# An AdaLN block with Mamba-2 layers and a mixture of experts: all input loads moved to the first slots of the DMA queue, the blank rows of the expert lists to later ones

## The chip, the core and the metric

The kernel runs on one core of a Trainium2 chip. A core has five engines with an instruction stream of their own each: PE (TensorE, matrix products), DVE (VectorE), ACT (ScalarE), POOL (GpSimd) and SP (SyncE), which here does nothing but issue transfers (DMAs). Transfers from SP, ACT and POOL stand in queues of their own and are carried out by 16 DMA engines that all queues share. Each engine takes its instructions in the order of the program; engines wait for one another, and for transfers, by semaphores. The metric is the time of one execution on the device, in microseconds (us); below are medians of several runs.

## The reference

Eight sequences (B=8) of 512 tokens (L) with 128 features (DM). Each goes through a modulated layer norm, four Mamba-2 layers with residuals, and a second modulated norm with a mixture of experts (8 experts, the best 2 for each token, and a shared one):

```python
mod = (silu(c) @ wmod).reshape(8, 6, 1, -1)       # sa, ca, ga, sb, cb, gb
h = layernorm(x) * (1 + ca) + sa
for l in range(4):                                # Mamba-2 layer
    z, xBC, dt = split(rmsnorm(h, w[l]) @ W_in[l])
    xBC = silu(causal_conv4(xBC, conv_w[l]) + conv_b[l])
    xs, Bm, Cm = split(xBC)
    dt = softplus(dt + dt_bias[l]); A = -exp(A_log[l])
    state = state * exp(dt * A) + (dt * xs) x Bm  # scan over 512 steps
    y = state . Cm + D[l] * xs
    h = h + rmsnorm(y * silu(z), gate_w[l]) @ W_out[l]
x = x + ga * rmsnorm(h, final_w)
h = layernorm(x) * (1 + cb) + sb
x = x + gb * (shared_expert(h) + top2_of_8_experts(h))
```

## The kernel before

**Tiles and units.** A sequence's input is one tile of 128 partitions by 4 chunks by 128 features (256 KB). One layer of one sequence is a unit, 32 in all (layer by layer, all eight sequences in each), and a unit has four chunks of 128 tokens (NC=4). The scan is done in chunks: 128 *items*, each one chunk of one unit, with a 128x128 decay matrix per head (the tile `dV`, 512 KB). Decay rows are computed for two units at a time (a group, eight items), stored to DRAM (`crow`), and loaded back broadcast over the partitions (`dV` and `ecum`).

**One hand-written order.** The whole scan part is one loop over *slots*, `for t in range(-NC * LEAD - EARLY, NI + 4)`, with `p = t + 16`. It runs from p=-9 (t=-25) to t=131. What a slot emits is each engine's order, and nothing is rearranged. In slot t are, among others: item t's products and state, the elementwise work of item t+1 to t+3, the loads of item t+4 (`decay_rows`, the `dV` load on SP), the projection and convolution of tile p, and one step of each generator in `gens`, in the order in which they were put there. A generator is a piece of work cut by `yield` into steps of one slot.

**Names in the prediction.**
- `enter(b)` (line 608) is the generator that takes sequence b in. It starts at p = 4b-9: x load on SP (line 613); a slot later the product `pmA` of `scb` and the modulation weights `wm` on PE (616), which ACT copies to `md` (618, 619), then layer norm: statistics on DVE (164, 166), the inverse root on POOL (149, 150), scaling (ACT line 181, or POOL 172), times scale and plus shift (185, 186), sums of squares on ACT (155), inverse root on POOL, normalizing (203 on ACT, or 201 on POOL: `hnA`), transposing on PE (208), and ACT's copy to `hT` (210). Sequences 1 to 4 use POOL for most of it (`idle`), the others ACT and DVE.
- `project_x` (PE, 638) writes tile `px` into one of three PSUM banks; `conv_first` (ACT, 650) and, a slot later, three taps `conv_tap` (DVE, 660) make `xbc` of it. `silu` (ACT, 672, 673) finishes a unit.
- `softplus_a` to `sums_b` (lines 693 to 767) make the decay of a group; line 765 stores `crow`. `decay_rows` (779 and 786) loads it, `decay_diff` on POOL (793) is the first to use a `dV` tile. There are six `dV` buffers, so that SP's load of item t+4 waits until PE has used the tile of item t-2 (line 920).
- `load_small()` (117) is a generator of three steps: `dtb`, `negA`; then four loads of `Dch` and `gw`; then `fw` and the FFN's norm weight. It starts at p=-4.
- `load_weights(l)` (595) loads `Wi` and `Wo` of a layer on SP, the first at p=-8. ACT's queue has the loads of `cT` and `wm` (92, 93), POOL's those of `bw`, `cw` and `cbias` (94 to 96).
- `clear_lists()` (243) writes blank rows into the lists `xg` of the experts in DRAM, from a tile `blank`: 64 transfers of 260 KB and one of 130 KB on SP. It starts at p=-2 (t=-18). The first 36 go out three a slot, to p=9; the other 29 one a slot, from p=10 to p=38 (t=22).
- `prepare_experts` (255), from p=0, computes modulations for the second half and loads its small parameters. `scale_weights(l)` (601, POOL) scales `Wo` in every 32nd slot.

After the scan the sequences are joined and routed, token rows are scattered to `xg` (from 824 us on), and 39 tiles of 256 rows go through the experts. The routing needs every blank row to be written.

SP issues the x loads and the blank rows in one queue with everything else: in a slot the step of `load_weights` comes first, then `decay_rows`, then the generators.

Of the kernel before, what the change touches and what calls it, by code (L numbers as in the profile page):

```python
# [15 lines left out]
P = 128  # L16
# [8 lines left out]
def adaln_mamba_moe(  # L25
# [27 lines left out]
    nc = tc.nc  # L53
    B, L, DM = x.shape
# [4 lines left out]
    NC = L // Q  # L59
# [97 lines left out]
    def layernorm_mod(xt, scale, shift, ht, name, on_pool):  # L157

        st = small.tile([P, NC, 6], F32, tag="st", name=f"st{name}")
        mv = small.tile([P, NC, 2], F32, tag="mv", name=f"mv{name}")  # L160
        rs = small.tile([P, NC], F32, tag="rs", name=f"rs{name}")
        off = small.tile([P, G2], F32, tag="poff", name=f"off{name}")[:, :NC]
        for s in range(NC):
            nc.vector.bn_stats(st[:, s, :], xt[:, s, :])
        for s in range(NC):
            nc.vector.bn_aggr(mv[:, s, :], st[:, s, :])
        yield
        rsqrt(rs, mv[:, :, 1], 1.0, 1e-5)
        if on_pool:
            eng = nc.gpsimd  # L170
            for s in range(NC):
                eng.tensor_scalar(
                    ht[:, s, :], xt[:, s, :], mv[:, s, 0:1], rs[:, s : s + 1], ALU.subtract, ALU.mult
                )
        else:
            eng = nc.vector
            nc.gpsimd.tensor_mul(off, mv[:, :, 0], rs)
            nc.gpsimd.tensor_scalar_mul(off, off, -1.0)
            yield
            for s in range(NC):  # L180
                nc.scalar.activation(
                    ht[:, s, :], xt[:, s, :], AF.Identity, bias=off[:, s : s + 1], scale=rs[:, s : s + 1]
                )
        yield
        eng.tensor_mul(ht, ht, scale.unsqueeze(1).to_broadcast([P, NC, DM]))
        eng.tensor_add(ht, ht, shift.unsqueeze(1).to_broadcast([P, NC, DM]))
        yield
# [25 lines left out]
    hTs, hp, xp, xs = {}, {}, {}, {}  # L213
# [29 lines left out]
    def clear_lists():  # L243

        n = 2 * TT
        for k, r in enumerate(range(0, E * ER + TT, n)):
            n = min(n, E * ER + TT - r)
            nc.sync.dma_start(
                xg[r : r + n, :].rearrange("(n p s) w -> p n (s w)", p=P, s=2),
                blank.rearrange("p s w -> p (s w)").unsqueeze(1).to_broadcast([P, n // TT, 2 * RW]),  # L250
            )
            if k % 3 == 2 or k >= 36:
                yield

    def prepare_experts(pool):

# [248 lines left out]
    def pbank(name):  # L505
        return psP.tile([P, 512], F32, tag="p", name=name)
# [66 lines left out]
    with ExitStack() as actx:  # L573
# [21 lines left out]
        def load_weights(l):  # L595
            Wi[l] = wip.tile([P, NPROJ], F32, tag="Wi", name=f"Wi{l}")
            nc.sync.dma_start(Wi[l], W_in[l])
            Wo[l] = wp.tile([P, NB, DM], F32, tag="Wo", name=f"Wo{l}")
            nc.sync.dma_start(Wo[l], W_out[l].rearrange("(k p) m -> p k m", p=P))
# [5 lines left out]
                nc.gpsimd.tensor_scalar_mul(dg[l][:, k, :], ident, Dch[:, l, k : k + 1])  # L605


        def enter(b):
            if b % 2 == 0:
                xp[b // 2] = fx.tile([P, 2, NC, DM], F32, tag="x", name=f"x{b}")  # L610
                hp[b // 2] = stay.tile([P, 2, NC, DM], F32, tag="h", name=f"h{b}")
            xs[b] = xt = xp[b // 2][:, b % 2]
            nc.sync.dma_start(xt, x[b].rearrange("(s p) d -> p s d", p=P))
            yield
            pm = pbank(f"pmA{b}")
            nc.tensor.matmul(pm[:, : 2 * DM], scb[:, b, :], wm[:, : 2 * DM], start=True, stop=True)
            md = norm.tile([P, 2, DM], F32, tag="md", name=f"mdA{b}")
            nc.scalar.copy(md[:, 0, :], pm[:, :DM])
            nc.scalar.activation(md[:, 1, :], pm[:, DM : 2 * DM], AF.Copy, bias=1.0)
            hs[b] = ht = hp[b // 2][:, b % 2]  # L620

            idle = 0 < b < 5
            yield from layernorm_mod(xt, md[:, 1, :], md[:, 0, :], ht, f"A{b}", idle)
            yield from rms_transposed(b, 1e-5, bw[:, 0:1], f"A{b}", pbank, htp, on_pool=idle)
            hT[b] = hTs.pop(b)

        def renorm(u):

            l, b = divmod(u, B)
            yield from rms_transposed(b, 1e-5, bw[:, l + 1 : l + 2], f"_{u}", pbank, htp, NC - 2)  # L630
            hT[u + B] = hTs.pop(b)
# [339 lines left out]
        def item(i):  # L971
            return 0 <= i < NI

        def unit(v):
            return 0 <= v < U
# [16 lines left out]
        EARLY = 9  # L992
        for t in range(-NC * LEAD - EARLY, NI + 4):
            p = t + NC * LEAD
            drain = p >= NI
            if p == 5 - EARLY:
                gens["small"] = load_small()
            if p == 0:
                gens["experts"] = prepare_experts(df)
            if p == 7 - EARLY:  # L1000
                gens["lists"] = clear_lists()
            if t == NI - LEAD * NC + 2:
                for k, w in enumerate((sw1, sw2.rearrange("(k p) o -> p k o", p=P))):
                    w12.append(wip.tile([P, NPROJ], F32, tag="Wi", name=f"ws{k}")[:, :FH])
                    dst = w12[k] if k == 0 else w12[k].rearrange("p (k o) -> p k o", o=DM)
                    nc.sync.dma_start(dst, w)
            for g, seqs in enumerate(sets):
                if t == NC * (U - B) + NC * (seqs[-1] + 1) + 2:
                    gens["pairs", g] = rejoin(g)
            v, j = divmod(p, NC)  # L1010
            vc, jc = divmod(p - 1, NC)

            if (p + 2 * NC) % (NC * B) == 0 and unit(p // NC + 2):
                load_weights((p // NC + 2) // B)
            if p % (NC * B) == NC and unit(v):
                scale_weights(v // B)
            if p == NC:
                nc.scalar.activation(negA, negA, AF.Exp)
                nc.scalar.mul(negA, negA, -1.0)
            if (p + EARLY) % NC == 0 and 0 <= (p + EARLY) // NC < B:  # L1020
                gens[(p + EARLY) // NC] = enter((p + EARLY) // NC)
            if t % NC == 3 and unit(t // NC - 1) and t // NC - 1 + B < U:
                gens[t // NC - 1 + B] = renorm(t // NC - 1)

            if item(t + 4):
                decay_rows(t + 4)
            vz, jz = divmod(p - 5, NC)
            if jz == 0 and unit(vz):
                silu(vz)
            if item(t + 2):  # L1030
                decay_exp(t + 2)

            if item(t):
                state_out(t)
            if item(t - 1):
                chunk_out(t - 1)
            if item(t):
                state_decay(t)
            if item(t + 1):
                weigh(t + 1)  # L1040
            if drain and scatters and item(t + 3):
                scatter(*scatters.pop(0)[1:])
            if item(t):
                mix(t)
            if item(t - 3):
                out_add(t - 3)
            if item(t):
                state_next(t)
            if drain:
                step_pairs()  # L1050
            if item(t - 1):
                gate(t - 1)
                square(t - 1)
            if item(t - 2):
                project_out(t - 2)
            if item(t + 1):
                gram(t + 1)
            if item(t + 2):
                transposes(t + 2)
            if item(t + 3):  # L1060
                decay_diff(t + 3)
                decay_mask(t + 3)
            if unit(vc):
                conv_tap(vc, jc, 1)
            if item(t - 2):
                out_scale(t - 2)
            if unit(vc):
                conv_tap(vc, jc, 2)
                conv_tap(vc, jc, 3)
                px.pop((vc, jc))  # L1070
            for key in list(gens):
                if not step(gens[key]):
                    del gens[key]
            if drain and routed:
                serve()
            group_stages(p, ((sums_a, 7),))
            if j == 1 and unit(v):
                project_dt(v)
            group_stages(p, ((softplus_a, 2), (softplus_b, 3), (softplus_c, 5), (softplus_d, 6), (sums_b, 7)))
            if unit(v):  # L1080
                project_x(v, j)
                conv_first(v, j)
            if j == 0 and unit(v - 1):
                project_z(v - 1)
# [245 lines left out]
```

## Time and profile before

| what | value |
|---|---|
| median of 3 runs | 1150.12 us (1149.14 to 1151.19) |
| the profiled execution | 1149.32 us, of it 1146.8 from the first to the last instruction |
| busy | PE 84%, DVE 75%, POOL 75%, ACT 66% of the span |
| granted PE clock | 0.932 on average; 0.67 from 20 to 35 us, 0.68 from 77 to 94, 0.89 from 94 to 147, 1.00 from 195 on |
| first item of the scan (DVE line 852) starts | 94.3 us |
| last item of the scan starts | 859.1 us |
| mean busy share of the DMA engines | 1.10 from 20 to 35 us, 1.11 from 50 to 60, 0.89 from 77 to 94, 0.36 to 0.45 in the scan |
| all blank rows | 65 transfers, 16.8 MB, issued from 17.4 to 228.8 us |
| all x loads | 8 transfers, 2 MB, issued from 0.8 to 112.9 us |

How to read it: before 94 us the pipeline is filled, and no engine is busy throughout; the 800 us after that are the scan, where each group of eight items takes the same time to a hundredth of a microsecond (45.2 us, or 46.8 where the weights of a layer are scaled); then come routing and experts. A DMA share over 1 comes from transfers that overlap in the records. In the prediction's lines "SPq" is SP issuing a transfer, `xg<-blank` names what is written and what it is read from, "x6" counts instructions that were merged in one line, and brackets hold the engine's idle time before the instruction and what ended it.

### The profile page before, as it was taken

The numbers are of one execution on the slowest core, as the hardware profiler recorded it, in microseconds if no ns is written. First come the engines' busy times: TensorE is split into PE (matmuls) and PEld (weight loads), VectorE is DVE, ScalarE is ACT, GpSimd is POOL, SyncE is SP. The second block draws the span as 40 slices with busy tenths as digits, with TensorE's granted clock in tenths as the row PEclk, the third lists the DMA queues.
The fourth block names the chain that finished last, engine by engine and source line by source line (L and its number), as shares of the span: only waits on it lengthen the run. The fifth ranks groups of instructions, "written<-read, shape, count | busy, mean of one in ns | idle before, by whom it ended". The sixth has DMA issues, their size and how long they took to land. (4 is left out here: it accounts for less than half of the span.)

```text
span 1146.8 us, 21570 instructions
## 1 busy us (share of the span) xinstructions
PE 964.2 (84%) x7130; PEld 730.3 (64%) x7130; DVE 856.5 (75%) x2084; ACT 761.1 (66%) x1641; POOL 855.9 (75%) x937
## 2 busy tenths in 40 slices
PE   3666899989999889999998999879664994999995
PEld 1234666766677667666666676657453673988882
DVE  2767888798988988988889888887764652666653
ACT  3676888888898788888978887876534741333320
POOL 6858889798898898988988988989666163555550
PEclk9777989999999999999999999986886896999997
DMA  6964536443253243343332434434201016877756
GB/s 154 235 164 158 181 100 188 132 133 110 85 162 110 87 140 109 108 128 107 121 110 87 141 109 125 134 91 131 86 26 37 6 47 156 227 225 224 222 153 224
DMA packets 134303, 151.19 MB, mean 132 GB/s; under 512 B 22569, under 2 KB 106697, under 8 KB 134193
## 3 DMA queue, kind: packets, MB, share of 16 engines
q1 hardware_dynamic: 127184, 137.91, 41.1%
q0 software_dynamic: 4672, 9.42, 2.5%
q10 hardware_dynamic: 2336, 2.50, 0.7%
q8 instruction: 56, 0.92, 0.3%
q14 instruction: 55, 0.44, 0.1%
HBM read 120.07 MB, written 29.71 MB: 131 GB/s over the span
## 5 line engine op out<-in xcount | busy, mean ns | idle before, releaser
L660 DVE SCALAR_TENSOR_TENSOR xbc<-px,cw,xbc 128x511 f32<-128x511 f32 (+2 forms) x384 | 286.2, 745 | 23.4 <-ACT xbc L650 16.3
L793 POOL TENSOR_TENSOR dV<-dV,cum 128x1024 f32<-128x1024 f32 x128 | 243.8, 1905 | 5.4 <-DMA dV<-crow 5.3
L852 DVE TENSOR_TENSOR dV<-dV,ptx 128x1024 f32<-128x1024 f32 x128 | 155.0, 1211 | 18.7 <-ACT xT L830 18.6
L798 POOL TENSOR_SCALAR_AFFINE_SELECT dV<-dV 128x1024 f32<-128x1024 f32 x128 | 142.6, 1114 | 9.3
L809 ACT ACTIVATE dV<-dV 128x1024 f32<-128x1024 f32 x128 | 134.5, 1051 | 14.5 <-POOL dV L798 14.1
L488 POOL DMA_INDIRECT yg<-y,ix x78 | 84.1, 1078 | 77.5 <-DVE y L1216 62.9
L936 ACT ACTIVATE sq<-g 128x256 f32<-128x256 f32 x128 | 53.0, 414 | 119.0 <-DVE g L932 105.1
L638 PE MATMUL px<-hT,Wi 128*128 128x512 f32 x192 | 103.6, 621 | 15.9 <-DVE xbc L660 14.5
L650 ACT ACTIVATE xbc<-px,cbias,cw 128x512 f32<-128x512 f32 x128 | 98.4, 769 | 27.2 <-PE px L638 25.6
L488 POOL DMA_INDIRECT xg<-row,ix x64 | 63.3, 989 | 50.4 <-ACT hds L524 29.7
L836 POOL TENSOR_TENSOR xd<-xT,dt 128x256 f32<-128x256 f32 x128 | 79.2, 619 | 27.3 <-ACT xT L830 26.9
L861 PEld LDWEIGHTS py<-xbc,st 128*128 128x128 f32 x384 | 59.8, 202 | 60.1 <-issue 47.3
L951 PE MATMUL po<-Wo,g 128*128 128x128 f32 x512 | 88.9, 297 | 0.0
L1198 ACT ACTIVATE hd<-ph,bs 128x256 f32<-128x256 f32 x78 | 32.7, 470 | 84.3 <-PE ph L1192 81.9
L920 PE MATMUL py<-dV,xd 128*32 128x128 f32 x2048 | 84.5, 284 | 0.0
L947 PEld LDWEIGHTS po<-ones,sq 128*128 128x128 f32 x512 | 67.6, 192 | 26.1 <-issue 23.4
L910 PEld LDWEIGHTS py<-xbc,dg 128*128 128x128 f32 x512 | 79.5, 202 | 7.0 <-issue 1.0
L848 PE MATMUL ptx<-xbc 128*128 128x128 f32 x256 | 55.8, 300 | 33.1 <-DVE dV L852 32.4
L910 PE MATMUL py<-xbc,dg 128*128 128x128 f32 x512 | 81.9, 285 | 0.0
L947 PE MATMUL po<-ones,sq 128*128 128x1 f32 x512 | 78.1, 256 | 0.5 <-ACT sq L936 0.5
L1192 PE MATMUL ph<-xt,w 128*128 128x256 f32 x312 | 75.9, 388 | 0.1
L1205 PE MATMUL pe<-w,hd 128*128 128x128 f32 x624 | 75.9, 275 | 0.0
(252 smaller groups left out, 2343.0 us busy)
## 6 DMA issues: line engine op xcount, KB each, us to landing
dV<-crow SPq DMA_DIRECT2D x128, 512.0 KB, 3.8
w<-in_L_ffn_ew_dram SPq DMA_DIRECT2D x78, 256.0 KB, 3.5
xg<-blank SPq DMA_DIRECT2D x64, 260.0 KB, 5.9
ecum<-crow SPq DMA_DIRECT2D x256, 48.0 KB, 3.4
rows<-xg SPq DMA_DIRECT2D x39, 130.0 KB, 3.3
b<-in_L_ffn_eb_dram SPq DMA_DIRECT2D x39, 64.0 KB, 3.8
x<-in_L_attn_x_dram SPq DMA_DIRECT2D x8, 256.0 KB, 6.9
md<-mods SPq DMA_DIRECT2D x8, 256.0 KB, 4.9
```

What stands on the lines that cost most here:

```text
L488: i = nc.gpsimd.indirect_dma_start(out=to, out_offset=bass.IndirectOffsetOnAxis(ap=ix, axis=0), in_=of, in_offset=None)
L638: nc.tensor.matmul(px[v, k][:, :L], Wi[l][:, c0 : c0 + P], hT[v], start=True, stop=True)
L650: nc.scalar.activation(xbc[v][:, k, :], px[v, k][:, :L], AF.Identity, bias=cbias[:, l, k : k + 1], scale=cw[:, l, k, KT - 1 : KT],)
L660: nc.vector.scalar_tensor_tensor(xbc[v][:, k, d:], px[v, k][:, : L - d], cw[:, l, k, KT - 1 - d : KT - d], xbc[v][:, k, d:], ALU.mult, ALU ...
L793: nc.gpsimd.tensor_tensor(dV[i], dV[i], cums[g][:, h0 : h0 + NH].unsqueeze(2).to_broadcast([P, NH, Q]), ALU.subtract)
L798: nc.gpsimd.affine_select(out=dV[i], in_=dV[i], pattern=[[0, NH], [1, Q]], compare_op=ALU.is_ge, fill=-200.0, base=0, channel_multiplier=-1,)
L809: nc.scalar.activation(dV[i], dV[i], AF.Exp)
L852: nc.vector.tensor_mul(Ms[i], Ms[i], pg.pop(i).unsqueeze(1).to_broadcast([P, NH, Q]))
L910: nc.tensor.matmul(py[i][:, k, :], dg[l][:, k, :], xbc[u][:, k, t], start=False, stop=True, skip_group_check=True,)
L920: nc.tensor.matmul(py[i][j * HD : (j + 1) * HD, k, :], xd[:, h, :], M[:, h, :], start=False, stop=True, skip_group_check=True,)
L947: nc.tensor.matmul(pp[:, 2 * DM + c : 2 * DM + c + 1], sq[:, k, :], ones[:, 0:1], start=(k == 0), stop=(k == NB - 1))
L951: nc.tensor.matmul(pp[:, c * DM : (c + 1) * DM], g[:, k, :], Wo[l][:, k, :], start=(k == 0), stop=(k == NB - 1))
```

## The change

It has three parts.

1. The x load leaves `enter` and becomes `load_x(b)`, which is called at the head of slots p=-9 to p=-2, one sequence a slot, before anything else that the slot emits. `enter` takes the tile that is there.
2. `load_small` starts one slot earlier, at p=-5. Sequence 4's input stands ahead of its first step, sequence 5's ahead of the second, sequence 6's ahead of the third, sequence 7's after it. The order on SP's queue becomes x0, x1, Wi, Wo, x2, x3, x4, `dtb`, `negA`, x5, `Dch` (4), `gw`, x6, `fw`, norm weight, x7; it was x0, Wi, Wo, x1, `dtb`, `negA`, `Dch` (4), `gw`, `fw`, norm weight, blanks with x2 to x7 between them.
3. `clear_lists` starts at t=8 and yields after every transfer: 65 slots, t=8 to t=72.

```diff
@@ clear_lists
-            if k % 3 == 2 or k >= 36:
-                yield
+            yield
@@ enter
-        def enter(b):
+        def load_x(b):
             if b % 2 == 0:
                 xp[b // 2] = fx.tile([P, 2, NC, DM], F32, tag="x", name=f"x{b}")
                 hp[b // 2] = stay.tile([P, 2, NC, DM], F32, tag="h", name=f"h{b}")
-            xs[b] = xt = xp[b // 2][:, b % 2]
-            nc.sync.dma_start(xt, x[b].rearrange("(s p) d -> p s d", p=P))
+            xs[b] = xp[b // 2][:, b % 2]
+            nc.sync.dma_start(xs[b], x[b].rearrange("(s p) d -> p s d", p=P))
+
+        def enter(b):
+            xt = xs[b]
             yield
@@ the loop over slots
-            if p == 5 - EARLY:
+            if 0 <= p + EARLY < B:
+                load_x(p + EARLY)
+            if p == 4 - EARLY:
                 gens["small"] = load_small()
             if p == 0:
                 gens["experts"] = prepare_experts(df)
-            if p == 7 - EARLY:
+            if t == 2 * NC:
                 gens["lists"] = clear_lists()
```

No instruction of a compute engine is added, removed or moved; the tiles of x and h are allocated once each, so nothing waits for a buffer.

## The prediction

> **What bounds the kernel now.** I read the page's head, then the list of waits for the first 160 us (the change touches nothing but transfers, and only a compute engine that waits for a transfer can gain), then the timelines of those places.
>
> ```profile
> span 1146.8 us, 21570 instructions
> DVE stA L164 <- DMA x<-in_L_attn_x_dram: 19.8, 3, 14.1
> POOL dV L793 <- DMA dV<-crow: 5.3, 2, 4.3
> ```
>
> In each wait: the engine and line, what it waited for, us in total, times, longest. Two kinds of waits can move, and they sum to 25.1 us. That is far more than can be won. The first 4.1 us for x are the very first input, which nothing precedes. What the rest is worth depends on what the waiting engine would have found to do.
>
> ```profile
> 17.40 4.25 SPq L248 DMA_DIRECT2D xg<-blank  x6
> 21.69 0.73 SPq L613 DMA_DIRECT2D x<-in_L_attn_x_dram  x1
> 24.73 0.78 ACT L650 ACTIVATE xbc<-px,cbias,cw 128x512 f32<-128x512 f32 x1
> 27.45 0.87 DVE L164 BATCH_NORM_STATS2 stA<-x 128x6 f32<-128x128 f32 x4 [14.11 <-DMA x<-in_L_attn_x_dram]
> 28.52 2.28 DVE L660 SCALAR_TENSOR_TENSOR xbc<-px,cw,xbc 128x511 f32<-128x511 f32 x3
> 28.69 0.19 POOL L149 TENSOR_SCALAR rsA<-mvA 128x4 f32<-128x4 f32 x1 [0.34 <-DVE mvA L166]
> 34.73 1.27 POOL L186 TENSOR_TENSOR h<-h,mdA 128x512 f32<-128x512 f32 x1
> 36.15 0.30 ACT L155 ACTIVATE unread<-h 128x128 f32<-128x128 f32 x1
> 57.06 0.87 DVE L164 BATCH_NORM_STATS2 stA<-x 128x6 f32<-128x128 f32 x4 [1.53 <-DMA x<-in_L_attn_x_dram]
> 58.59 1.91 ACT L673 ACTIVATE xbc<-xbc 128x2048 f32<-128x2048 f32 x1
> 61.63 0.78 ACT L650 ACTIVATE xbc<-px,cbias,cw 128x512 f32<-128x512 f32 x1 [1.13 <-PE px L638]
> 77.20 1.90 POOL L793 TENSOR_TENSOR dV<-dV,cum 128x1024 f32<-128x1024 f32 x1 [4.30 <-DMA dV<-crow]
> 129.04 1.90 POOL L793 TENSOR_TENSOR dV<-dV,cum 128x1024 f32<-128x1024 f32 x1 [1.04 <-DMA dV<-crow]
> ```
>
> The columns are start, us, engine, line. Read it from the top: SP issues six blank transfers, and sequence 2's input only at 21.69, behind them. DVE stands at that input until 27.45, and the conv taps (L660) of the first tile, ready since ACT's L650 at 25.51, stand behind it in DVE's order. But ACT at 36.15 squares an h that POOL finished at 36.00: there POOL, not DVE, decides.
>
> **The x loads: cost of the stall removed.** Sequence 2's input is issued in slot -7 of p, some 3 us into the run, and DVE's statistics fall into its idle time after 13.34. So L660 can start at 25.51 instead of 28.52: 3.0 us at DVE. Follow it on. POOL's chain for sequence 2 starts when POOL has finished hnA (26.01+2.35=28.36), instead of 28.69: it gains 0.3. From there POOL runs unbroken to 36.00, and ACT's squares wait for it, so ACT keeps 0.3 of the 3.0. From 36.15 to 53.5 ACT has work nearly without a break (squares, three table loads of 1.28, silus of 1.91), and the 0.3 stays 0.3. The second stall is sequence 4 (57.06, 1.53 idle). With its input there, DVE's statistics run straight after the taps before them, L660 of the next tile ends before 59, and PE's px is no longer held back by the bank. ACT's L650 then starts not at 61.63 but when ACT is free: L673 ends at 60.50, less the 0.3, makes 60.2. That is 1.4 us. After it DVE, PE and ACT release one another in turn (softplus, the sums, crow at 70.91), with nothing else late: sequence 4's h on POOL gains about 1.9 and doesn't clip it. The first dV load follows crow, and POOL's wait for it at 77.20 is the latency of crow and dV one after the other; it stays 4.3 and starts 1.4 earlier. From 77.2 POOL is busy without a gap to 105.7, so the scan begins **1.4 us** earlier. Bounds: 0.3 (only POOL's share carries on) to 4.4 (3.0+1.4, if nothing clips). I take 1.4, the place where I can name the clipping engine.
>
> **The blanks taken out of the front.** Before, 36 blanks go out three a slot from p=-2, and 29 more one a slot to t=22; beside the x loads they cost compute only at POOL's second wait (129.04): the dV load of item 8 shares the queue with the blank issued 0.4 us behind it. After, no blank goes out before t=8, that load is issued in slot t=4, and dV's median of 3.8 us to landing (against 5.2 there: issue 123.67, wait ended about 128.9) ends the 1.04. POOL then runs without a gap to 136.7, where DVE waits 0.64 for POOL's st, and on to 143.3. So the worth is 0.64 to 1.04; I take **0.9**.
>
> **The blanks put into the scan.** 65 transfers, one in each slot t=8..72. Their price can be read directly, since t=8..22 had them before. The second group below has no blank, and both hold a scaling of Wo by POOL (line 604), so they compare:
>
> ```profile
> L852 DVE TENSOR_TENSOR dV<-dV,ptx x9: 1210/1211/1212, 195.0 to 241.9; 128x1024 f32<-128x1024 f32 x9
> L852 DVE TENSOR_TENSOR dV<-dV,ptx x9: 1209/1210/1212, 377.5 to 424.3; 128x1024 f32<-128x1024 f32 x9
> 195.00:241.90 46.90, 42.40 (x364) 31.57 (x355) 39.84 (x86) 38.60 (x77) 40.78 (x47) 1.00 0.45 140
> 377.50:424.30 46.80, 42.31 (x364) 31.55 (x352) 39.73 (x85) 38.51 (x77) 41.07 (x47) 1.00 0.35 109
> SPq L779 <- PE py L920: 163.0, 43, 6.5
> ```
>
> Eight slots took 46.9 us with the last six blanks beside them and 46.8 without (DMA share, second last column, 0.45 against 0.35). The cover is SP's own waiting: from 161 to 560 us it stands 163 us for dV buffers, and a blank goes out behind that wait. Behind the blank in SP's order are only the next dV and ecum loads, and POOL showed no DMA wait in that stretch at all. Price 0; upper bound 0.1 for each of the six groups that get blanks anew, **0.6**. If the cover went, a late first dV load of a group would stall POOL one for one, six times.
>
> **What is moved behind the x loads.** Seven loads of 256 KB now stand ahead of most small parameters and the second one ahead of Wi. Six of them are 1.5 MB, at the 318 GB/s that the queues moved between 4 and 7 us some 5 us. Needed are: Wi at 19.9 (PE's px), dtb at 31.05 (DVE L687), gw and Dch at 36.5 and 37.09 (POOL), fw at 39.35, negA at 39.82. Dch was issued until 9.74 and takes 12.0 to landing: 9.7+5+12=27 is early enough. POOL's own queue (cw, cbias) is needed at 24.73 by ACT; between 17 and 36 us every packet is of SP's queue, so it was done by 17, and 5 us more is early enough too. The eight SP issues themselves (0.47 each) replace eight later ones.
>
> **The one that isn't covered is wm**, the modulation weights, on ACT's queue: PE's first product starts at 7.63 when they land, and the whole front hangs on that product, through ACT's h at 9.19 and POOL at 14.15. Any delay counts in full. Before, Wi (388 KB) was issued just ahead of wm (1.30 and 1.32); after, x of sequence 1 (256 KB) is. From 5.0 to 6.2 us:
>
> ```profile
> q10 hardware_dynamic: 123, 0.35, 77.3%
> q1 hardware_dynamic: 104, 0.06, 16.2%
> ```
>
> (packets, MB, share.) SP's queue (q1) had Wo and x issued since 2.3, and still moved next to nothing while wm (q10) passed: the two went one after the other, in the order of issue. 132 KB less ahead of wm is 0.4 us at 318 GB/s, less what smaller packets cost; I take **0.2** gained, between 0.4 gained and 5.7 lost (if wm took Dch's 12.0 to landing: 13.3 for 7.6).
>
> The Trainium skill speaks against it here ("DMA: Bandwidth & Descriptors", section "Queues, rings and completion order"): each DMA engine takes turns, packet by packet, between the queues it has work for. By that rule wm would share with the flood of x and take up to twice its 1.2 us, an estimate of 1.0 more, and the sum would be 1.5 won rather than 2.5. The row above shows turns not being taken evenly; it decides.
>
> **Sum.** 1.4 + 0.9 + 0 + 0.2 = 2.5 us off a span of 1146.8: 1144.3. The profiled execution took 1149.32 (2.5 lie around the span) and stands 0.8 under the median of three, 1150.12. Median after: **1147.6**. A measurement of this kernel can't tell less than 0.2%, 2.3 us, from no change, so the forecast lies at that edge.
>
> **Rivals.** (a) *Hidden anyway*: POOL's order keeps 0.3 of the front, or a half-clock stretch eats the rest (the granted clock was 0.68 from 77 to 94 us, 0.89 from 94 to 147, and which stretches run slow depends on when PE is idle). For it: the 14.1 us stall shrinks to 0.3 already in my own sum. Against: the 57.06 stall has no other work under it. Time 1150.1-0.3-0.6=1149.2. (b) *More comes back*: the 3.0 at DVE isn't clipped at 36.15, since PE and ACT get room earlier. For it: DVE's taps are dense from 33.8 to 55.5. Against: POOL's unbroken run. 4.4+0.9 makes 1144.8. (c) *Slower*: the flood of x delays wm. Place: PE's first product, 7.63. It decides from a landing 4.8 us later on (2.3 won otherwise, and 2.3 lost to be told): past 12.4. Small loads behind data took 12.0 to land, so wm at 13.3 costs 5.7-2.3=3.4: 1153.5. Against: wm is issued behind one x only. Late dV loads in the six groups (2 us each, less 2.5, is 9.5 more) belong to the same side and speak against themselves in the two group rows.
>
> **Chances.** Forecast 0.50 (own range 1146 to 1149; about 0.32 of it beyond the 0.2%), (a) 0.20, (b) 0.16, (c) with its like 0.14. Faster by over 0.2%: 0.32+0.16=0.48; within: 0.18+0.20=0.38; slower 0.14. Range 1144.0 to 1151.5: below it part of (b), above it (c).
>
> **What would show it.** Right: one wait of DVE for x is left (4.1 us); first taps near 25.3, crow's store near 69.3; POOL's wait for dV at about 75.6 still 4.3, and none near 127; eight slots of the scan still 45.2 or 46.8; wm's product near 7.4. Wrong: wm's product past 8.5, ACT waiting for cw or cbias, POOL waiting for Dch, or a DMA wait of POOL between 280 and 520 us. If crow's store moves by 0.3 alone, (a) is right; by 3 or more, (b).

## The result and the profile after

The changed kernel takes 1149.18 us in the median of twelve runs (1147.42 to 1155.04); the kernel before, run beside it on the same chip, 1149.57 (1145.88 to 1153.02). The ratio is 1.0002 with a 95% interval of 0.9987 to 1.0017: no difference that this measurement can tell. 1147.6 was forecast, 2.5 us ahead of before: a ratio of 0.9978, which lies outside this interval. The profiled execution took 1151.86 us, of it 1150.2 between the first and the last instruction, above the median of its own runs; that of before lay a little under its own. So the two spans are compared stretch by stretch and not as wholes.

First the lines of the page's head and the list of waits of the changed kernel that answer to those of before (engine and line, what was waited for, us in total, times, longest):

```profile
span 1150.2 us, 21566 instructions
...
DVE stA L164 <- DMA x<-in_L_attn_x_dram: 4.4, 1, 4.4
POOL dV L795 <- DMA dV<-crow: 5.5, 1, 5.5
```

DVE's waits for x fell from 19.8 us in three to the first alone, which nothing precedes. POOL's waits for dV went from two to one, but that one grew, from 4.3 to 5.5 us. Then the timeline of the front, changed kernel (start, us, engine, line):

```profile
6.55 2.08 PE L618 MATMUL pmA<-wm,scb 128*128 128x256 f32 x4 [6.55 <-DVE scb L115]
...
23.96 0.78 ACT L652 ACTIVATE xbc<-px,cbias,cw 128x512 f32<-128x512 f32 x1
24.78 2.32 DVE L662 SCALAR_TENSOR_TENSOR xbc<-px,cw,xbc 128x511 f32<-128x511 f32 x3 [11.16 <-ACT xbc L652]
35.01 0.31 ACT L155 ACTIVATE unread<-h 128x128 f32<-128x128 f32 x1 [2.90 <-POOL h L186]
54.77 0.86 DVE L164 BATCH_NORM_STATS2 stA<-x 128x6 f32<-128x128 f32 x4
60.47 0.77 ACT L652 ACTIVATE xbc<-px,cbias,cw 128x512 f32<-128x512 f32 x1
69.73 0.70 SPq L767 DMA_DIRECT2D crow<-ct  x1
73.23 0.82 SPq L781 DMA_DIRECT2D dV<-crow  x2
77.24 1.90 POOL L795 TENSOR_TENSOR dV<-dV,cum 128x1024 f32<-128x1024 f32 x1 [5.51 <-DMA dV<-crow]
127.43 1.90 POOL L795 TENSOR_TENSOR dV<-dV,cum 128x1024 f32<-128x1024 f32 x1
```

The first product starts 1.08 us earlier, the first taps (28.52 before) 3.74, ACT's squares (36.15) 1.14, the first convolution of sequence 4's second tile (61.63) 1.16, the store of crow 1.18. And POOL multiplies the first dV at 77.24, where it did so at 77.20. Everything won by 69.73 is gone by 77.24. In between lies one transfer: the dV load waits for crow in DRAM, and is issued 3.50 us after the store. Before, the same pair of lines reads:

```profile
70.91 0.70 SPq L765 DMA_DIRECT2D crow<-ct  x1
73.08 0.35 SPq L779 DMA_DIRECT2D dV<-crow  x1
```

That is 2.17 us. The store took 1.33 longer, and that is the first item of the account. POOL's wait at item 8 (127.43) is gone, as forecast. The spans of both profiled executions, divided at the starts of DVE's mix (line 852, now 854), us:

| stretch | before | after | difference |
|---|---|---|---|
| start to the first item | 94.26 | 94.29 | +0.03 |
| items 0 to 8 | 53.09 | 52.30 | -0.79 |
| items 8 to 16 | 47.68 | 48.42 | +0.74 |
| items 16 to 24 | 46.82 | 46.83 | +0.01 |
| items 24 to 32 | 45.21 | 46.31 | +1.10 |
| items 32 to 48 | 90.42 | 90.44 | +0.02 |
| items 48 to 56 | 46.82 | 47.93 | +1.11 |
| items 56 to 112 | 319.94 | 319.90 | -0.04 |
| items 112 to 127 | 114.86 | 114.86 | 0.00 |
| last item to the end | 287.69 | 288.87 | +1.18 |

The two groups that grew by 1.10 had blanks put into them, and so had items 32 to 48, 56 to 64 and 64 to 72, which didn't grow. One slot holds all of the growth in each: items 26 and 50. The windows over those two places (us, busy time of PE, weight loads, DVE, ACT and POOL with counts, then granted PE clock, DMA share and GB/s):

```profile
252.50:255.90 3.40, 3.40 (x12) 2.51 (x10) 2.74 (x7) 3.03 (x7) 3.19 (x4) 0.50 0.21 74
389.00:392.40 3.40, 3.40 (x9) 2.19 (x9) 2.57 (x7) 3.30 (x8) 2.75 (x3) 0.50 0.29 104
```

PE is busy from end to end at half its clock, the DMA share is 0.21 and 0.29 (0.35 and 0.45 in the groups before the change), and POOL waits for no dV there: these are not late transfers.

The last stretch is left open. From the last item to the end it took 301 to 311 us on two of the chips (the first four runs below and the last one) and 287 to 291 on the others, in kernels with and without the change; in those five runs nothing after the last item is compared.

### The profile page after: what moved, and what is told of

Its sections match the earlier page's. It is cut to its first block, busy times and chain, and to the rows that moved or that the text cites. A ratio compares the mean times of both kernels' runs of the same rounds, so it can differ in the third digit from the quotient of the medians.

```text
span 1150.2 us, 21566 instructions
## 1 busy us (share of the span) xinstructions
PE 967.3 (84%) x7130; PEld 732.4 (64%) x7130; DVE 859.0 (75%) x2084; ACT 761.5 (66%) x1641; POOL 856.3 (74%) x937
## 5 line engine op out<-in xcount | busy, mean ns | idle before, releaser
L863 PEld LDWEIGHTS py<-xbc,st 128*128 128x128 f32 x384 | 60.3, 204 | 60.6 <-issue 47.4
L949 PEld LDWEIGHTS po<-ones,sq 128*128 128x128 f32 x512 | 67.7, 192 | 26.1 <-issue 23.2
```

The lines of the kernel that those rows point to most:

```text
L949: nc.tensor.matmul(pp[:, 2 * DM + c : 2 * DM + c + 1], sq[:, k, :], ones[:, 0:1], start=(k == 0), stop=(k == NB - 1))
```

## The experiments

### One part of the change at a time

Two theories stood for the store: the loads moved ahead make it slow (a queue that has become idle, or traffic of theirs), or something else happens to lie on it. And the parts of the change had to be told apart. So both kernels were looked at again, and each half of the change was made alone (the small loads, one slot earlier, went with the x loads).

The changed kernel as it is:

> The changed kernel, profiled a second time. Theory A (a collision by chance): the first store of crow is issued at 69.7 us again, as compute sets that, but its landing (3.5 us after issue in the first profile, 2.1 in the kernel before) depends on whether PE's 16 KB fetch of instructions (at 70.9 in the first profile) meets it; landing 2.1 to 3.5, and the first scan item at 93.0 to 94.3. Rival B (the store is always late without blanks around it, an idle queue): 3.5 again, first item at 94.3. In the scan, slots t=26 and t=50 were 1.1 us long each at half clock: theory A' (the place of the clock's 3.41 us windows against the slots): other slots of the same kind (t = 2 mod 8) are long this time, or none; rival B' (the blanks cause it): t=26 and t=50 again.

The kernel before as it is:

> The kernel before, profiled a second time. First taps of the convolution at 28.5 us, crow's first store issued at 70.9 and landed 2.1 later unless PE's fetch meets it, first scan item at 94.3. If the clock's windows lie by chance (A'), slots of t = 2 mod 8 can be 1.1 us long here too, blanks or not; if the blanks cause it (B'), none from t=24 to t=104, as in the first profile.

Only the x loads moved, the blanks as before:

```diff
+            if 0 <= p + EARLY < B:
+                load_x(p + EARLY)
...
             if p == 7 - EARLY:
                 gens["lists"] = clear_lists()
```

> Only the x loads moved; blanks as before (36 of them three a slot from p=-2). If the x loads are what ends the stalls: first taps near 24.8 us, no wait of DVE for x but the first (4.4), crow issued near 69.7, and POOL's second wait for dV (1.04 near 128) is still there, since blanks stand beside that load. If the blanks in the front cost something of their own, crow comes later than 69.7.

Only the blanks moved, the x loads as before:

```diff
-            if k % 3 == 2 or k >= 36:
-                yield
+            yield
...
-            if p == 7 - EARLY:
+            if t == 2 * NC:
                 gens["lists"] = clear_lists()
```

> Only the blank rows moved to t=8 to 72; x loads in enter as before. If the x inputs were late only because blanks stood ahead of them: x of sequence 2 lands before 25.5, first taps at 25.5, x of sequence 4 lands before 56, crow near 69.5 to 70.0, so nearly all of the change's gain in the front without moving x. wm lands at 7.5 as before (first product 7.6). If the x loads have to be early themselves: first taps after 26.5 and crow at 70.5 or later. POOL's wait of 1.04 near 128 is gone either way.

One run each: 1174.04, 1167.64, 1159.07 and 1169.9 us, beside 1164.62 for before. The traces say more than these times (us; "store" is crow's, issue and the time until the dV load behind it can go; "fetch" is explained below):

| | first product | ACT's first h | first taps | store issued, took | fetch starts | first mix |
|---|---|---|---|---|---|---|
| before | 7.63 | 9.19 | 28.52 | 70.91, 2.15 | 70.0 | 94.26 |
| before again | 7.32 | 8.88 | 28.32 | 70.29, 3.68 | 71.5 | 95.12 |
| after | 6.55 | 8.42 | 24.78 | 69.73, 3.48 | 70.9 | 94.29 |
| after again | 8.54 | 10.11 | 26.46 | 71.48, 3.70 | 72.7 | 96.31 |
| x loads alone | 6.56 | 8.43 | 24.79 | 68.96, 2.14 | 67.7 | 92.37 |
| blanks alone | 7.59 | 9.15 | 25.53 | 70.02, 3.16 | 71.2 | 94.68 |

Three things follow. *The stall of DVE came from the blanks.* Taken from ACT's first h, the first taps come at 16.36 us after the change and at 16.38 with the blanks alone (19.33 before). Where x stood in SP's order mattered only because the blanks stood ahead of it; DVE still waits 8.8 us for it there, and this wait costs nothing. *The slow store isn't the change's.* It took 3.68 in the kernel before on its second look, and 2.14 with the x loads moved. That second look at before, on SP:

```profile
70.29 0.70 SPq L765 DMA_DIRECT2D crow<-ct  x1
73.99 0.35 SPq L779 DMA_DIRECT2D dV<-crow  x1
```

*Something else lies on the store.* The share of the DMA engines while it ran in the changed kernel, from 70.8 to 72.3 us (queue, packets, MB, share of 16 engines):

```profile
q1 hardware_dynamic: 138, 0.06, 20.5%
q8 instruction: 1, 0.02, 5.4%
```

One packet of q8, the queue that fetches instructions for an engine, takes 5.4% of 16 engines for 1.5 us: 1.3 us of one DMA engine. It begins 1.2 us after the store's issue, and the store, whose packets go to all the engines, isn't complete before this one has moved its share. The trace shows it at the store's completion, which is reported in 16 steps: 15 of them came by 2.16 us after the issue, and the last alone at 3.48, 1.0 us after the fetch had ended. In before the fetch began 0.9 us ahead of the store's issue, with the x loads alone 1.3 ahead. That made a theory to be tested: the packet is PE's, since it comes at the same place of PE's instruction count (109 or 112 instructions in). In these six profiles DVE's count at that moment is as steady (110 to 112), so they alone don't tell the two engines apart; the run with products, below, does.

*The front before the store.* From ACT's first h to the store it is 61.72 us before, 61.31 after, 60.53 with the x loads alone. The last two differ by one group of products, on PE's timeline. After, then the x loads alone:

```profile
54.61 3.52 PE L646 MATMUL pz<-hTA,Wi 128*128 128x512 f32 x4
```

```profile
54.58 2.13 PE L647 MATMUL pz<-hTA,Wi 128*128 128x512 f32 x4
```

The windows of 51.1 to 57.9 us have a granted clock of 0.50 after and of 0.71 with the x loads alone. The store came 0.77 us later for it: at the start of these products the two timelines still agree to 0.03 us, and ACT's `silu` behind them starts 0.77 later. Where the half-clock stretch falls differs between executions of the same code. The x loads alone, looked at a second time below, took 3.52 for these products and 61.30 from ACT's first h to the store. And the second look at before took 61.41, 0.31 less than the first.

### Moving the fetch, swapping the loads ahead of wm, more blanks

Six products into two banks that nothing reads move PE's instruction stream on:

```diff
+            if b == 0:
+                for r in range(2):
+                    spare = psO.tile([P, 512], F32, tag="o", name=f"spare{r}")
+                    for _ in range(3):
+                        nc.tensor.matmul(spare[:, : 2 * DM], scb[:, b, :], wm[:, : 2 * DM], start=True, stop=True)
```

> The changed kernel with six products more at the start of the front, into two banks that nothing reads (they leave nothing out). They move PE's instruction stream on by 24 instructions, so that its next instruction fetch falls some microseconds earlier. Theory 'collision': the store of crow for sequence 0 took 3.48 us to land after the change only because PE's instruction fetch (1.3 us on one DMA engine) began 1.2 us after the store was issued; with the fetch 3 us or more ahead of the store, the store lands in 2.1 to 2.3 us, the first mix follows 24.6 us after crow's issue less 1.3 (23.3 instead of 24.6), and the scan begins 1.3 us earlier. Rival 'something of the change itself makes the store slow' (the loads of x, an idle queue): the store still takes 3.2 to 3.7 us although no fetch lies on it. Both theories: the time to the end of the run scatters by 1 to 3 us through half-clock slots, so I expect the ratio to before within 0.998 to 1.001.

The fetch began at 60.6, and the store took 2.16 us. SP's timeline:

```profile
69.50 0.70 SPq L772 DMA_DIRECT2D crow<-ct  x1
71.68 0.82 SPq L786 DMA_DIRECT2D dV<-crow  x2
```

The first mix started at 93.05, that is 1.24 us ahead of the changed kernel, 23.55 after the store (24.56 there). The theory of the collision holds, and the fetch is PE's: it came 107 of PE's instructions in, near the 109 and 112 above, but only 95 of DVE's and 93 of ACT's in, against 110 to 112 and 106 to 112 there. The time over twelve runs was 1148.73 us, ratio 0.9982 (0.9961 to 1.0004): not told from no change.

The x loads alone, timed:

> Only the loads of x moved ahead, the blanks as before (a second and timed look at the same code as the run with the x loads alone). Theory 'the front gain is real and survives where no fetch lies on the store': the first mix at 92.4 us (94.3 in before), wm landed at 6.3 to 6.6, ratio to before 0.998 to 0.999 over five rounds. Rival 'half-clock slots decide': the first mix is earlier by 1 to 2 us again, but the ratio is within 0.001 of 1. Rival 'wm is at the mercy of the load of x ahead of it': wm lands at 8 us or later in some profile, and then the first mix comes no earlier than 94.

Ratio 0.9992 (0.9970 to 1.0015), and a first mix at 94.56: neither the 92.4 of its first look nor the second theory's gain. Both reasons were seen above, now in the same code: the pz products took 3.52 us, and the store was issued at 69.72 instead of 68.96; then the fetch began at 71.1, 1.4 us behind the store's issue, and the store took 3.37. wm landed at 6.5, so the third theory is not seen here. Whether fetch and store meet differs from run to run of one kernel.

The input of sequence 1 behind Wi and Wo:

```diff
-            if 0 <= p + EARLY < B:
+            if 0 <= p + EARLY < B and p + EARLY != 1:
                 load_x(p + EARLY)
...
                 load_weights((p // NC + 2) // B)
+            if p + EARLY == 1:
+                load_x(1)
```

> The changed kernel, but the input of sequence 1 is loaded after the two weights Wi and Wo, so that Wi stands ahead of wm in the order of issue as in before. Theory 'the transfer issued just ahead of wm decides when wm lands': wm lands at 7.2 to 7.5 us, PE's first product starts at 7.3 to 7.6 and ACT's first h at 8.9 to 9.2 (6.3, 6.6 and 8.4 with x ahead). Rival 'order plays no part': wm still at 6.3 to 6.6, or at 8.4 as in one look. Everything after it shifts with the first product; the stalls for x stay away in both (one wait of DVE for x, 4 to 5 us).

PE's first product:

```profile
7.64 2.05 PE L618 MATMUL pmA<-wm,scb 128*128 128x256 f32 x4 [7.64 <-DMA wm<-in_L_wmod_dram]
```

With Wi ahead wm lands at 7.50 as it did before; with the input of sequence 1 ahead at 6.3 to 6.6 in all profiles but one. What is issued just ahead of wm decides. The exception is the second look at the changed kernel, where wm landed at 8.41: 15 of its 16 completion steps had come by 6.36, and the last one was late, which stays open. Yet the store was issued at 69.69 here and at 69.73 in the changed kernel, although ACT's first h came 0.78 later (9.20). The pz products tell why:

```profile
55.31 2.19 PE L646 MATMUL pz<-hTA,Wi 128*128 128x512 f32 x4
```

They took 2.19 us here and 3.52 in the changed kernel, so a half-clock stretch there took back what wm had won. Beside the x loads alone in their first look, where pz took 2.13, first h and store come 0.77 and 0.73 later here: with pz alike, the gain at wm reaches the store.

Every blank three times:

```diff
+            for _ in range(3):
-            nc.sync.dma_start(
+                nc.sync.dma_start(
```

> The changed kernel with each blank transfer issued three times, so that slots t=8 to 72 hold three transfers in place of one (nothing left out; the same rows are cleared three times). Theory 'the blanks are covered by SP's waiting': the groups of eight slots without a half-clock slot still take 45.2 and 46.8 us, POOL waits for no dV load in the scan except where the margin was thin (items 42 and 74, 0.47 and 0.70 us to spare), at most 0.5 us at each, so at most 1 us in all. Rival 'each blank costs something': the groups between t=8 and t=72 get longer by 0.1 us or more each, or POOL's waits for dV sum to over 2 us.

1373.6 us, 224 more than the changed kernel: the first theory fails, the second has the sign but not the size, and the reason is in the list of waits:

```profile
SPq L249 <- DMA xg<-blank: 381.1, 130, 5.1
...
POOL dV L796 <- DMA dV<-crow: 265.4, 63, 7.3
```

A transfer to rows that another is still writing waits for it by a semaphore that stands in the program just ahead of it on SP, 130 times, 2.9 us each in the mean. SP stands there, the dV loads queue up behind it, and POOL waits for them 265 us. So this was no test of three transfers. It shows what a wait in SP's order costs where a transfer alone costs nothing. Three transfers a slot without such waits follow below.

### The half-clock slots, and three different blanks a slot

In all profiles the records of PE's clock change on a grid of 3.413 us that runs through the whole execution. When each slot starts on this grid was set against its length. Long slots are those 1.10 us over their like. In the first six profiles, from item 18 to 106, they came only among the slots t = 2 mod 8, and only where these started at 0.22 to 0.29 of the grid's period. To test it, work was added ahead of item 20, which moves what follows against the grid:

```diff
             if item(t):
+                if t == 20:
+                    for _ in range(2):
+                        nc.vector.tensor_scalar_mul(dV[t], dV[t], 1.0)
                 mix(t)
```

> The changed kernel with two products of dV by one (128x1024, in place, the values stay the same) on DVE ahead of the mix of item 20: work added to the scan, 1.2 to 2.2 us on DVE, of which DVE's idle 1.3 us after item 21 may swallow a part. Theory 'a slot t = 2 mod 8 takes 1.10 us more when and only when it starts at 0.22 to 0.29 of the clock's 3.413 us window': the profiles of the changed kernel start slot 26 at 0.22 or 0.23, and slots 26, 50 and 106 are long. If the added work makes slot 26 start later by d, the rule gives: d of 0.3 to 0.5 us: only slot 74 long; 0.6 to 0.8: none, so that items 16 to 112 take 3.3 - d less than after (2.5 to 2.7 us less although work was added); 0.9 to 1.1: slots 50 and 106 and perhaps 98; 1.35 to 1.65: none again. Rival 'the long slots belong to this kernel's transfers' (blanks): 26, 50 and 106 stay long whatever d is.

The same with `range(4)`:

> As the run with two products of dV by one, but four: 2.4 to 4.4 us on DVE, of which 1.3 us or more may be swallowed. By the clock rule, with d the delay of slot 26 against the changed kernel: d of 1.35 to 1.65 us or 2.4 to 2.55: no long slot at all; 1.8: slots 42 and 82; 1.95: 42 and 98; 2.1: 58; 2.25: 106; 2.7: 34 and 74. Rival 'the long slots belong to the blanks': 26, 50 and 106 whatever d is.

With two products items 16 to 26 took only 0.07 us more: nearly all of the added work was swallowed, and slot 26 started at 0.24 of the period (0.22 without). Slots 26, 66 and 106 were long, which started at 0.24, 0.25 and 0.26; slot 50, at 0.30, was not. With four it started at 0.66. Then 26, 50 and 106 all kept their usual length, and slot 42, at 0.26, was long (as was slot 100, by 1.12, of which the rule says nothing). For this delay, 1.5 us, no long slot at all had been expected; slot 34 took 0.35 us more than its like and so moved slot 42 into the range. The window where the changed kernel has its first half-clock slot, now:

```profile
252.50:255.90 3.40, 2.94 (x25) 2.60 (x22) 3.21 (x10) 3.37 (x5) 3.33 (x4) 1.00 0.64 175
```

and the one over the start of slot 42:

```profile
346.40:349.80 3.40, 3.40 (x10) 2.21 (x10) 2.58 (x8) 3.34 (x8) 2.81 (x3) 0.50 0.26 93
```

The blanks stood in the same slots in all three kernels, so the long slots aren't theirs. The profiles of the halves say the same: with the blanks alone moved none of these slots was long, and in the timed look at the x loads alone, with the blanks as before, 26, 50 and 106 were. Over the thirteen profiles (that of every blank three times over left out), 22 of the 156 slots t = 18, 26, ..., 106 were long: all of those that started at 0.19 to 0.29, and none of the others. The lower edge was guessed too high: 0.18 was not long, 0.19 was. The Trainium skill ("TensorE: Matmul & The Clock Gate", section "Part 1: The HAM clock gate (the "warmup" mystery)") gives the window of PE's clock gate as 3413 ns and says that it runs freely and doesn't start anew with a kernel. The profiles agree: in the two looks at before, the same code, the first record began 13.9 and 11.9 us behind PE's first product, and the 2.1 between them is no multiple of the period. One run each: 1149.17 us with two products and 1153.68 with four, beside 1152.19 for before. With two the span was 1147.0 us, 3.2 shorter than the changed kernel's profile, though items 16 to 112 took 0.5 longer: items 120 to 127 took 63.6 instead of 66.9.

Three different blanks a slot, so that none waits for another:

```diff
-            yield
+            if k % 3 == 2:
+                yield
```

> The changed kernel with three different blank transfers in each slot from t=8, so that all 65 are out by t=29 (nothing left out; no row is cleared twice, so that no blank waits for another, which is what the run with every blank three times over added). Theory 'transfers cost nothing while SP has waiting to spare': items 16 to 24 take 46.8 us and POOL waits for no dV load from t=16 to t=30, or at most 1 us in all. Rival 'two more transfers a slot are no longer covered': items 16 to 24 take 0.5 us or more longer, and POOL shows waits for dV there.

POOL's waits from 180 to 360 us, in which the changed kernel has none for dV:

```profile
POOL dV L796 <- DMA dV<-crow: 11.0, 5, 4.0
```

Items 16 to 24 took 48.35, of which 1.11 is a half-clock slot (18, at 0.27), and items 32 to 40 took 48.48 instead of 45.22. Two transfers more a slot are not covered: the second theory holds. At one a slot the cover is there, and it is no wide one. From 180 to 290 us SP's waits for dV buffers fell from 44.4 us in the changed kernel to 6.7, but the share of the DMA engines rose from 0.55 to 0.83 as well; which of the two makes the dV loads late isn't told apart. This run shows the store once more with the front's code unchanged. The fetch began at 68.8, ahead of it:

```profile
69.78 0.70 SPq L768 DMA_DIRECT2D crow<-ct  x1
71.95 0.82 SPq L782 DMA_DIRECT2D dV<-crow  x2
```

The store was issued 0.05 us later than in the changed kernel's profile, and the dV load behind it 1.28 earlier. In the fourteen profiles the store took 2.14 to 2.16 us in the five where the fetch began ahead of it, and 3.16 to 3.70 in the nine where it began 1.2 to 1.6 us behind its issue. In each of these nine, 15 of the store's 16 completion steps came by 2.16 us and one alone was late, and the dV load went out 0.95 to 1.12 us after the fetch's packet had ended, however long that was (0.96 to 1.47). So the wait ends with the fetch. Whether the change makes the meeting likelier isn't settled: with the x loads moved and no PE products added it came in seven of nine profiles, in before in one of two.

### The version with the fetch moved, once more

> The version with the fetch moved (the changed kernel and six products that nothing reads at the start), timed once more against before, since 0.9982 [0.9961, 1.0004] leaves open whether it is ahead. Theory 'the store's 1.3 us and the item 8 wait come through to the end': ratio 0.997 to 0.999; the store of crow lands in 2.1 to 2.3 us again and the first mix starts at 92.9 to 93.2. Rival 'the half-clock slots, whose number depends on how the scan meets the clock's windows, scatter more than that': ratio 0.999 to 1.001, with the store at 2.1 to 2.3 all the same. If the fetch lands on the store again (3.2 us or more), the products do not place it and the first run was chance.

The store took 2.15 us, the first mix started at 93.08, and the ratio was 1.0002 (0.9980 to 1.0023). The products place the fetch, and that isn't enough to beat the kernel before by what can be measured. No version here does.

## Why the prediction was right or wrong

**The x loads, -1.4 forecast.** Right up to the squares of ACT: they came 1.14 earlier, of which 0.77 is ACT's earlier first h, so 0.37 came by way of POOL, where 0.3 was worked out; DVE's 3.0 was clipped there as described. From then on it failed, in two places. "After it DVE, PE and ACT release one another in turn ... with nothing else late": PE was late, its pz products at half clock took 3.52 us, and of 1.4 only 0.41 reached the store in the changed kernel's profile, counted from ACT's first h (1.19 with the x loads alone, where the half-clock stretch lay elsewhere; pz took 2.07 in before). As this stretch took 61.72 and 61.41 in the two looks at before, and 60.49 to 61.45 in the eleven profiles with the x loads moved, even the 0.41 is no firm size. And "it stays 4.3 and starts 1.4 earlier": the wait for crow and dV did not stay. It was taken as a fixed latency, while it holds the time of a store that PE's instruction fetch can lengthen by 1.0 to 1.6 us; it did so after and didn't in the profile of before. This is the step that cost the forecast its front. The Trainium skill ("DMA: Bandwidth & Descriptors", section "Queues, rings and completion order"), weighed in the prediction at wm, bears on this place instead: if a DMA engine takes turns between its queues by whole packets, a store can lose the whole turn of the other queue, here a packet of 1.0 to 1.5 us, and 1.0 to 1.6 was lost.

**The blanks out of the front, -0.9.** The mechanism was right and so was its size: the wait at item 8 went, and items 0 to 8 took 0.79 less. The next group gave 0.74 back: the slot of item 11 took 1.1 longer, with a half-clock stretch from 167.1 to 170.5. Unforeseen was that moving the blanks alone does nearly all that moving x does at DVE.

**The blanks in the scan, 0.** Right. In the changed kernel POOL waits for no dV from 78 us to the end, and the groups without a half-clock slot have their old lengths to 0.02 us. The bound of 0.1 a group came from the rounding of its two windows: at DVE's mix both groups took 46.82. The cover named, SP's waiting, fits the runs: where SP itself had to wait 381 us for blanks (every blank three times over), POOL waited 265 us for dV. That this waiting alone is the cover isn't shown, since with three different blanks a slot the DMA engines were fuller too.

**wm, -0.2.** The direction and the order of issue were right, the size was not: the product started 1.08 earlier, ACT's first h 0.77. The sum by bytes (132 KB less at 318 GB/s) was too small. The row that was read as turns not being taken evenly, from 5.0 to 6.2 us, is uneven in bytes (0.35 to 0.06 MB), while its packets are 123 to 104: it doesn't speak against turns by packets. In one look of the changed kernel it went the other way, by 0.9, to 8.54: rival (c) in small, and just past the 8.5 that was named as a sign of being wrong. What was won did reach the store where the pz products ran alike (0.73 of 0.77); in the changed kernel's own profile their half-clock stretch took it back.

**The sum.** -2.5 was forecast to reach the end. In the profile -1.2 was there at the store and +0.03 at the first item. The range, 1144.0 to 1151.5, held the measured 1149.18, but it also held no change at all; the forecast's own 1146 to 1149 just missed it. So that it held says nothing for the sum, of which nothing was left at the first item. Of the rivals, (a), 1149.2, hit the time; half of its reason, a half-clock stretch that eats the rest, was seen in the pz products and in slots 26 and 50. Those two slots are also long in three more profiles with the input of sequence 1 ahead of wm; in the kernel before only slot 106 or none was. Whether the change makes that pattern likelier isn't settled: other profiles with the same loads have others. (b) did not come, since POOL clips as worked out, and (c) in its full size did not either.

## What to carry to other kernels

A term of a sum that ends at a store or load needs the time of that transfer in more than one execution: its one measured latency can include or miss an instruction fetch on the same DMA engine. Where PE runs dense, a shift of a microsecond changes which products fall into a half-clock window, and this can be worth as much as the shift; a gain of 0.2% in the front is then to be looked for at the stretch where it was made, and believed at the end only with many runs. And before moving a load ahead of what delays it, try moving what delays it: here moving the blanks alone brought the first taps and removed the wait at item 8 just as the whole change did.

## What the runs showed of the hardware

- One 16 KB instruction fetch of PE occupied a DMA engine for 0.9 to 1.5 us, and a 64 KB store that met it took 3.16 to 3.70 us instead of 2.15: 15 of its 16 completion steps came in time, and the last about 1.0 us after the fetch had ended.
- The granted clock of PE changed on a grid of 3.413 us, whose place against the first product differed between executions of the same code. Slots that started at 0.19 to 0.29 of its period took 1.10 us more, in 22 of 22 cases, and none of the other 134 did.
